# A batch norm's statistics taken out of the opening stage and placed among the steps of the first super tile

## The chip, the cores and the metric

One Trainium2 chip; the program runs on one of its cores. The metric is the device time of an execution in microseconds (us), smaller being better. The engines are TensorE (PE; PEld is its weight load), VectorE (DVE), ScalarE (ACT), GpSimd (POOL), and SyncE (SP), which issues most DMA transfers. Each engine works through its own instructions in order and waits on semaphores for the others.

## The reference

Two layers over x of shape (2, 2048, 256), in float32. The first adds two branches to x, both fed by a layer norm: a state space block, and a mixture of small experts found by product keys. The part that the change touches is the batch norm in front of the key search:

```python
xn = _layernorm(x, axis=-1)
x = x + _L0_attn_ref(xn, ...) + _L0_ffn_ref(xn, ...)
...
q = (hidden_states @ Wq + bq).reshape(B, S, H, QD)      # in _L0_ffn_ref, hidden_states = xn
mean = q.mean(axis=(0, 1, 2))
var = q.var(axis=(0, 1, 2))
q = (q - mean) / jnp.sqrt(var + EPS_BN) * bn_gamma + bn_beta
q0 = _l2norm(q[..., :HALF])
q1 = _l2norm(q[..., HALF:])
```

The mean and variance run over all 4096 rows and 8 heads, so they must be known before the first query is normalised. The state space block normalises xn a second time. The second layer is causal attention plus a mixture of 8 routed experts.

## The kernel before

The 4096 rows are 32 tiles of 128 rows (`NT`), four tiles to a super tile (`TPS`), eight super tiles (`NST`). All of x stays in on-chip memory (`xr`).

**The opening stage** (lines 235 to 464) holds its scratch tiles in one pool (`s_k`) and its matmul results in two others. Instead of computing all queries twice, it gathers the Gram matrix of the normalised rows, of 256 x 256 with a column of sums, and derives the queries' mean and variance from it:

- `measured(t)` (line 285): VectorE takes mean and variance of the rows of a tile.
- `scaled(st)` (294): GpSimd turns them into scale s1 and bias b1 of the first layer norm, four small instructions for each super tile.
- `products(st)` (301): ScalarE writes the normalised rows of four tiles into one of two buffers xg, and TensorE adds their products to two accumulators, psg (L309) and psh (L310).
- `scaled_twice(st)` (312): GpSimd computes scale s2 and bias b2n for the second normalisation, and s1p, in seven instructions with a scratch tile r2 (L316 to L322).
- `powers()` (335): a generator whose steps, small matmuls with VectorE copies, build the powers of the state matrix; its later steps build lt (L360, L365) and bw (L370, L374). One step is taken after every second tile of `measured`.

The loop over super tiles (387) calls `measured` and a `powers` step for the tiles of super tile st, then `scaled(st)`, then `products(st - 1)`. Within this stage the order on TensorE, VectorE, ScalarE and GpSimd is the order written. Behind the loop come a memset of a 128 x 2064 region of zeros (`zero`, a part of the tile xnT1 that is not used yet; line 403), `scaled_twice` for the first four super tiles, the keys' transpose (408), and then the batch norm's chain (413 to 464):

- gm (414, 415): the accumulators scaled; its missing block by a transpose (417, 418);
- wgw (423, 426): gm times the query weights, times the weights;
- psm (432, 436): 32 one-column matmul pieces, which give mean and second moment by column;
- mq, dev, acc1 (442 to 447), a matmul that averages over the heads (449), the deviations (451 to 455), a second such matmul (457), the root on GpSimd (459), and bn_a, bn_b (462 to 464), which `queries_taken` (729) uses.

The other four `scaled_twice` stand behind the root on GpSimd. Behind the stage SyncE sends `zero` five times to a buffer in device memory (467).

**The super tiles' stage.** Every step of a super tile is a small function with a start time in a table (`PLAN`, and `ENDING` for the last super tile). `at(st, f, ...)` (493) puts it on a list with the time st * 68.0 + start, and the sorted list (1483) is the order of TensorE, VectorE, ScalarE and GpSimd; the times only sort. The opening of super tile 0 reads: `rows_twice` (ScalarE, with s2 and b2n), `rows_twice_turned` (TensorE transposes, L193), `rows_twice_taken` (ScalarE, into xn2T), `x_part` (TensorE, L553, xn2T times the input weights), `inputs` (L541), `ends` (L594), `scan_round` (L606), and further on `queries` (L725). New pools, `l0_k` for scratch among them, are opened for this stage in the memory that the opening stage's pools give back.

Of the kernel before, what the change touches and what calls it, by code (L numbers as in the profile page):

```python
# [9 lines left out]
F32 = mybir.dt.float32  # L10
I32 = mybir.dt.int32
AF = mybir.ActivationFunctionType
ALU = mybir.AluOpType
AX = mybir.AxisListType
# [3 lines left out]
P = 128  # L18
B, L, D = 2, 2048, 256
T = B * L  # L20
NT = T // P
SW = 512
NST = T // SW
TPS = SW // P
SPB = L // SW
EPS = 1e-5

DI, DS, DC = 512, 16, 4
NI = DI // P
# [23 lines left out]
    products=((82.01, 79.31), (94.08, 92.53), (114.32, 113.41), (129.20, 128.99)),  # L53
# [6 lines left out]
ZW = 2064  # L60
RW = D + 2
NOROW = 1.0 * 2 ** 20

ENDING = dict(
    rows_twice=(-41.22, -13.33, -40.66, -17.29), rows_twice_turned=(-6.87, 0.70), rows_twice_taken=(-0.20, 1.41),
# [32 lines left out]
PH, PQ, PK = 8, 64, 32  # L98
# [19 lines left out]
PP_GAMMA, PP_BETA, PP_CW, PP_CB, PP_BQ, PP_BNG, PP_BNB, PP_RB, PP_QROW, PP_B1 = 0, 2, 4, 20, 24, 28, 29, 30, 34, 38  # L118
PP_N = PP_B1 + E * NF

M_ID, M_TRI, M_ONE, M_MASK, M_AVG, M_SEL = range(6)
# [3 lines left out]
def layers_kernel(  # L125
# [32 lines left out]
    V, S, G, PE = nc.vector, nc.scalar, nc.gpsimd, nc.tensor  # L158
# [8 lines left out]
    mats = keep.tile([P, 6, P], F32, name="mats")  # L167
    pp = keep.tile([P, PP_N], F32, name="pp")
    small = keep.tile([P, 20 + NT], F32, name="small")
    nhalf = keep.tile([P, 64], F32, name="nhalf")  # L170
# [9 lines left out]
    ident = mats[:, M_ID, :]  # L180

    def col(c, n=1):
        return pp[:, c:c + n]
# [12 lines left out]
    with tc.tile_pool(name="xt", bufs=1) as xt:  # L196

        xnT1 = xt.tile([P, 2, T], F32, name="xnT1")


        with ExitStack() as c3, ExitStack() as c2, ExitStack() as c1:
# [5 lines left out]
            wq_sb = mp.tile([P, 2, PH * PQ], F32, name="wq_sb")  # L207
# [12 lines left out]
            bn_a = wp.tile([P, 1], F32, name="bn_a")  # L220
            bn_b = wp.tile([P, NI], F32, name="bn_b")
# [13 lines left out]
            with ExitStack() as c0:  # L235
                wk = c0.enter_context(tc.tile_pool(name="s_k", bufs=1))
                ps1 = c0.enter_context(tc.tile_pool(name="s_p1", bufs=1, space=PSUM))
                ps2 = c0.enter_context(tc.tile_pool(name="s_p2", bufs=2, space=PSUM))
# [62 lines left out]
                def products(st):  # L301
                    for t in range(st * TPS, (st + 1) * TPS):
                        a = xg[st % 2][:, t % TPS, :]
                        S.activation(
                            a[:, 0:D], xr[:, t, :], AF.Identity, bias=b1[:, t:t + 1], scale=s1[:, t:t + 1]
                        )
                    for t in range(st * TPS, (st + 1) * TPS):
                        a = xg[st % 2][:, t % TPS, :]
                        PE.matmul(psg, a[:, 0:P], a, start=(t == 0), stop=(t == NT - 1))  # L309
                        PE.matmul(psh, a[:, P:D], a[:, P:], start=(t == 0), stop=(t == NT - 1))  # L310

                def scaled_twice(st):

                    ts, m, v, h = of_tile(st)
                    r2 = wk.tile([P, TPS], F32, name="r2", bufs=2)
                    G.tensor_tensor(r2, v, s1[:, ts], ALU.mult)  # L316
                    G.tensor_tensor(r2, r2, s1[:, ts], ALU.mult)
                    G.tensor_scalar(r2, r2, EPS, None, ALU.add)
                    G.tensor_tensor(r2, r2, h, ALU.pow)
                    G.tensor_tensor(s2[:, ts], s1[:, ts], r2, ALU.mult)  # L320
                    G.tensor_tensor(b2n[:, ts], b1[:, ts], r2, ALU.mult)
                    G.tensor_scalar(s1p[:, ts], s1[:, ts], 1.0, None, ALU.add)  # L322
# [61 lines left out]
                kt = wk.tile([P, P], F32, name="kt")  # L384
                k2 = wk.tile([P, 1], F32, name="k2")
                todo = powers()
                for st in range(NST + 1):
                    for t in range(st * TPS, min(st + 1, NST) * TPS):
                        measured(t)
                        if t % 2:  # L390
                            next(todo, None)
                    if st < NST:
                        scaled(st)
                    if st:
                        products(st - 1)
                    if st == NST - 2:
                        V.tensor_tensor(kt, kn, kn, ALU.mult)
                        V.tensor_reduce(k2, kt, AX.X, ALU.add)
                        V.tensor_scalar(k2, k2, 1e-24, None, ALU.max)
                        G.tensor_tensor(k2, k2, nhalf[:, 0:1], ALU.pow)  # L400
                for _ in todo:
                    pass
                G.memset(zero, 0.0)
                for st in range(NST // 2):
                    scaled_twice(st)
                V.tensor_scalar(kn, kn, k2, None, ALU.mult)
                ps = ps1.tile([P, SW], F32, tag="mm", name="ps_mm")
                PE.transpose(ps[:, :P], kn, ident)
# [1 line left out]

                gm = wk.tile([P, 2, D + 1], F32, name="gm")
                V.tensor_scalar(gm[:, 0, :], psg, 1.0 / T, None, ALU.mult)
                V.tensor_scalar(gm[:, 1, P:], psh, 1.0 / T, None, ALU.mult)
                ps = ps1.tile([P, SW], F32, tag="mm", name="ps_mm")
                PE.transpose(ps[:, :P], gm[:, 0, P:D], ident)
                V.tensor_copy(gm[:, 1, 0:P], ps[:, :P])
                wgw = wk.tile([P, 2, PH * PQ], F32, name="wgw")
                for o in range(2):  # L420
                    ps = ps2.tile([P, SW], F32, tag="h", name="ps_gw")
                    for dc in range(2):
                        PE.matmul(
                            ps, gm[:, dc, o * P:(o + 1) * P], wq_sb[:, dc, :], start=(dc == 0), stop=(dc == 1)
                        )
                    V.tensor_tensor(wgw[:, o, :], ps, wq_sb[:, o, :], ALU.mult)
                psm = ps1.tile([P, 2 * NI], F32, tag="st", name="ps_st")
                one = mats[:, M_ONE, 0:1]
                for m in range(NI):
                    ms = slice(m * P, (m + 1) * P)  # L430
                    for dc in range(2):
                        PE.matmul(
                            psm[:, m:m + 1], wq_sb[:, dc, ms], gm[:, dc, D:], start=(dc == 0), stop=(dc == 1)
                        )
                    for dc in range(2):
                        PE.matmul(
                            psm[:, NI + m:NI + m + 1], wgw[:, dc, ms], one, start=(dc == 0), stop=(dc == 1)
                        )
                mq = wk.tile([P, 2 * NI], F32, name="mq")
                acc1 = wk.tile([P, 4], F32, name="acc1")  # L440
                dev = wk.tile([P, NI], F32, name="dev")
                V.tensor_copy(mq, psm)
                V.tensor_tensor(dev, mq[:, 0:NI], mq[:, 0:NI], ALU.mult)
                V.tensor_tensor(mq[:, NI:], mq[:, NI:], dev, ALU.subtract)
                V.tensor_scalar(mq[:, NI:], mq[:, NI:], 0.0, None, ALU.max)
                V.tensor_tensor(mq[:, 0:NI], mq[:, 0:NI], col(PP_BQ, NI), ALU.add)
                V.tensor_reduce(acc1[:, 0:1], mq[:, 0:NI], AX.X, ALU.add)
                ps = ps1.tile([P, 2 * NI], F32, tag="st", name="ps_st")
                PE.matmul(ps[:, 0:1], mats[:, M_AVG, :], acc1[:, 0:1], start=True, stop=True)
                mean = wk.tile([P, 1], F32, name="mean")  # L450
                V.tensor_copy(mean, ps[:, 0:1])
                V.tensor_scalar(dev, mq[:, 0:NI], mean, None, ALU.subtract)
                V.tensor_tensor(dev, dev, dev, ALU.mult)
                V.tensor_tensor(dev, dev, mq[:, NI:], ALU.add)
                V.tensor_reduce(acc1[:, 1:2], dev, AX.X, ALU.add)
                ps = ps1.tile([P, 2 * NI], F32, tag="st", name="ps_st")
                PE.matmul(ps[:, 0:1], mats[:, M_AVG, :], acc1[:, 1:2], start=True, stop=True)
                V.tensor_scalar(acc1[:, 2:3], ps[:, 0:1], EPS, None, ALU.add)
                G.tensor_tensor(acc1[:, 2:3], acc1[:, 2:3], nhalf[:, 0:1], ALU.pow)
                for st in range(NST // 2, NST):  # L460
                    scaled_twice(st)
                V.tensor_tensor(bn_a, acc1[:, 2:3], col(PP_BNG), ALU.mult)
                V.tensor_scalar(bn_b, col(PP_BQ, NI), mean, bn_a, ALU.subtract, ALU.mult)
                V.tensor_scalar(bn_b, bn_b, col(PP_BNB), None, ALU.add)

            for n in range(E * CAP * RW // (P * ZW)):
                nc.sync.dma_start(buf_z[n], zero)
# [23 lines left out]
            plan = []  # L491

            def at(st, f, *args):
                start = (PLAN if st < NST - 1 else ENDING)[f.__name__]
                for n in args:
                    start = start[n]
                plan.append((st * PERIOD + start, len(plan), f, args))

            def mamba(st):
                b = st // SPB  # L500
# [1185 lines left out]
```

## Time and profile before

| | before |
|---|---|
| median of 4 runs | 2087.78 us |
| lowest to highest | 2084.13 to 2089.53 us |
| profiled execution, its own time | 2087.93 us |
| its span | 2086.2 us |
| instructions | 38155 |
| TensorE busy | 2023.2 us, 97% of the span |
| VectorE, ScalarE, GpSimd busy | 1443.3, 1069.4, 598.2 us |
| keys' transpose on TensorE | 45.90 us |
| first `x_part` of super tile 0 | 61.16 us |

A row of the timeline gives the start in us, the duration, the engine, the line, the operation, the tile written and those read, the shape, how often it was repeated and, in brackets, how long the engine stood idle before it and what released it. Times on TensorE are pipelined: one matmul may start before the listed end of the one ahead, so distances of starts say more than durations. The granted clock is TensorE's, as a share of full speed.

### The profile page before, as it was taken

What the parts mean: (1) busy time and instruction counts of PE and PEld (TensorE: products, weight loads), DVE (VectorE), ACT (ScalarE), POOL (GpSimd) and SP (SyncE); (2) the same over time, 40 slices, a digit from 0 to 9 for tenths busy, and PEclk for the clock granted to TensorE, in tenths of its full rate; (3) what the DMA queues carried; (4) which work ended last, traced back from release to release, by engine and by line L of the source; (5) the groups of instructions that cost most, each with busy time, mean ns of one, the idle gap of its engine ahead of it and who ended that gap; (6) DMA issues with size and microseconds to landing.
All of it is one profiled execution on the core that took longest, in us unless ns stands there. A gap on an engine that the chain in (4) does not pass through costs nothing. (4 is left out here: it accounts for less than half of the span.)

```text
span 2086.2 us, 38155 instructions
## 1 busy us (share of the span) xinstructions
PE 2023.2 (97%) x14094; PEld 1031.5 (49%) x14094; DVE 1443.3 (69%) x4920; ACT 1069.4 (51%) x2028; POOL 598.2 (29%) x971
## 2 busy tenths in 40 slices
PE   7999999999979999999999999999999999999997
PEld 6455666565544343433333333433333333678786
DVE  4288898888996887777877788878878773211110
ACT  4576777676611345545555655565555657221211
POOL 5234555446573301310211102111011010332321
PEclk9999999999976999999999999999999999999999
DMA  6000000000121401210110101101200001433320
GB/s 230 28 1 1 11 6 6 11 11 9 39 89 49 91 7 42 60 25 32 33 30 17 45 27 43 37 17 26 75 10 10 7 10 49 144 116 101 111 72 13
DMA packets 64731, 90.82 MB, mean 44 GB/s; under 512 B 19640, under 2 KB 47606, under 8 KB 62880
## 3 DMA queue, kind: packets, MB, share of 16 engines
q1 hardware_dynamic: 58960, 76.75, 12.7%
q0 software_dynamic: 5376, 10.59, 1.6%
q8 instruction: 110, 1.80, 0.4%
q10 hardware_dynamic: 208, 1.05, 0.2%
q14 instruction: 77, 0.63, 0.1%
HBM read 56.53 MB, written 32.02 MB: 42 GB/s over the span
## 5 line engine op out<-in xcount | busy, mean ns | idle before, releaser
L1280 ACT ACTIVATE pt<-ps_p 128x512 f32<-128x512 f32 (+3 forms) x1280 | 608.1, 532 | 501.9 <-PE ps_p L1232 347.8
L1232 PE MATMUL ps_p<-kT,qT 32*128 32x512 f32 (+3 forms) x2560 | 717.2, 585 | 7.0 <-DVE mx L1243 6.0
L1275 PE MATMUL ps_p<-qT,kT 32*128 32x512 f32 (+3 forms) x2560 | 630.5, 575 | 1.7 <-DVE t L1150 0.8
L1248 DVE TENSOR_REDUCE mx<-ps_p 128x1 f32<-128x512 f32 x768 | 491.7, 685 | 133.6 <-PE ps_p L1232 93.5
L1282 POOL TENSOR_SCALAR_AFFINE_SELECT pt<-pt 128x128 f32<-128x128 f32 x512 | 143.8, 292 | 808.9 <-ACT pt L1280 800.7
L1300 PE MATMUL ps_av<-pt,va 128*32 128x256 f32 (+1 forms) x4608 | 351.8, 379 | 4.0 <-POOL pt L1282 2.8
L1275 PEld LDWEIGHTS ps_p<-qT,kT 32*128 32x128 f32 x2560 | 204.7, 184 | 231.4 <-issue 170.3
L1232 PEld LDWEIGHTS ps_p<-kT,qT 32*128 32x128 f32 x2560 | 257.0, 186 | 46.1 <-ACT pt L1280 22.6
L1300 PEld LDWEIGHTS ps_av<-pt,va 128*32 128x32 f32 x4608 | 92.3, 108 | 375.8 <-issue 210.2
L1243 DVE CUSTOM_DVE_ANT_0 ps_p<-ps_p,mask_w 128x384 f32<-128x384 f32 (+3 forms) x512 | 241.4, 515 | 52.6 <-PE ps_p L1232 37.2
L1564 ACT ACTIVATE hT<-ps_h,pp 128x640 f32<-128x640 f32 x64 | 50.8, 794 | 222.1 <-PE ps_h L1560 222.1
L1578 PE MATMUL ps_eo<-w_sb,hT 128*128 128x256 f32 x640 | 141.8, 379 | 0.0
L1560 PE MATMUL ps_h<-xeT,w_sb 128*128 128x320 f32 x512 | 139.1, 432 | 0.0
L1578 PEld LDWEIGHTS ps_eo<-w_sb,hT 128*128 128x128 f32 x640 | 120.5, 190 | 16.7
L553 PE MATMUL ps_mm<-xn2T,w_in_sb 128*128 128x512 f32 x256 | 124.0, 607 | 0.0
L1560 PEld LDWEIGHTS ps_h<-xeT,w_sb 128*128 128x128 f32 x512 | 97.2, 190 | 39.6
L1582 DVE SCALAR_TENSOR_TENSOR eo<-ps_eo,xe,rs 128x256 f32<-128x256 f32 x40 | 19.4, 484 | 135.2 <-PE ps_eo L1578 135.2
L849 POOL TENSOR_TENSOR prod<-prod 128x1024 f32<-128x1024 f32 x32 | 75.2, 2351 | 82.8 <-DVE prod L839 80.6
L811 DVE MATCH_REPLACE8 mr<-m,sc 128x36 f32<-128x36 f32 x512 | 84.9, 176 | 0.0
L1583 POOL DMA_INDIRECT out_x<-eo,row x40 | 39.4, 985 | 151.5 <-DVE eo L1582 141.6
L839 DVE TENSOR_TENSOR prod<-e,ex 128x1024 f32<-128x1024 f32 x64 | 79.4, 1262 | 0.3
L1243 DVE DVE_READ_ACCUMULATOR2_ANT mx<- 128x1 f32 x512 | 72.6, 142 | 0.1
(270 smaller groups left out, 2528.7 us busy)
## 6 DMA issues: line engine op xcount, KB each, us to landing
w_sb<-in_w SPq DMA_DIRECT2D x16, 1024.0 KB
qk_d<-rot SPq DMA_DIRECT2D x16, 512.0 KB
tab<-in_c_tab SPq DMA_DIRECT2D x8, 768.0 KB
buf<-xnT SPq DMA_DIRECT2D x5, 1032.0 KB
xe<-buf SPq DMA_DIRECT2D x8, 645.0 KB
xr<-in_x SPq DMA_DIRECT2D x8, 512.0 KB
res<-xr SPq DMA_DIRECT2D x8, 512.0 KB
out_x<-xr SPq DMA_DIRECT2D x8, 512.0 KB
```

The source lines that it names most:

```text
L553: PE.matmul(ps, w_in_sb[:, dc, m * P:(m + 1) * P], h["xn2T"][:, dc], start=(dc == 0), stop=(dc == 1))
L811: V.match_replace(out=mr[:, g, :], in_to_replace=h["m8", k][:, g, :], in_values=sc2[k % 2][:, g, :], imm_value=GONE,)
L839: V.tensor_tensor(prod, h["e0", k][:, hs, :].unsqueeze(3).to_broadcast([P, PH // 2, 8, PK]), h["e4", k][:, hs, 1, :].unsqueeze(2).to_broad ...
L1232: PE.matmul(ps[:, :w], qT[u][r, qt * P:(qt + 1) * P], kT[u][r, kc * SW:kc * SW + w], start=True, stop=True)
L1243: V.tensor_tensor_reduce(out=ps[:, :w], in0=ps[:, :w], in1=a["mask"][:, SW - w:], scale=1.0, scalar=2 * MASKED, op0=ALU.add, op1=ALU.max, ...
L1248: V.tensor_reduce(to, ps[:, :w], AX.X, ALU.max)
L1275: PE.matmul(ps[:, c0:], kT[u][r, kt * P:(kt + 1) * P], qT[u][r, qb * SW + c0:(qb + 1) * SW], start=True, stop=True,)
L1280: S.activation(p[:, c0:], ps[:, c0:], AF.Exp, scale=HD ** -0.5)
L1282: G.affine_select(out=p[:, c0:c0 + P], in_=p[:, c0:c0 + P], pattern=[[1, P]], compare_op=ALU.is_ge, fill=0.0, base=0, channel_multiplier=-1,)
L1300: PE.matmul(av[u, qb][32 * j:32 * j + 32, lo:hi], va_of(b, g)[:, kt, v0:v0 + 32], pt[n, j][:, lo:hi], start=(kt == half == 0), stop=(kt == ...
L1560: PE.matmul(ps[:, hf, :HC], w1_sb[:, dc, f * P:(f + 1) * P], xeT[:, dc, hf * HC:(hf + 1) * HC], start=(dc == 0), stop=(dc == 1),)
L1578: PE.matmul(ps, hT[:, f, c * P:(c + 1) * P], w2_sb[:, f, :], start=(f == 0), stop=(f == NF - 1))
```

## The change

Two things. In the loop, `products` is called two super tiles behind `measured`, not one. And the batch norm's chain behind the scaling of the accumulators leaves the opening stage: its steps become fourteen entries of the list of super tile 0, with start times of their own (`NORM`). gm and wgw now lie in regions of xnT1 that are not used yet; mq, dev, acc1 and mean are tiles of the pool `l0_k`, and the matmul results take buffers of the super tiles' stage. All eight `scaled_twice` stand in a row behind the loop, ahead of the memset of `zero`.

```diff
+NORM = (-9.0, -8.9, -8.8, -8.7, -8.6, -8.5, -8.4, -1.0, -0.9, 2.9, 3.0, 11.0, 11.7, 13.0)
 ...
-                for st in range(NST + 1):
-                    for t in range(st * TPS, min(st + 1, NST) * TPS):
+                for st in range(NST + 2):
+                    for t in range(min(st, NST) * TPS, min(st + 1, NST) * TPS):
                         measured(t)
 ...
-                    if st:
-                        products(st - 1)
+                    if st > 1:
+                        products(st - 2)
 ...
+                for st in range(NST):
+                    scaled_twice(st)
                 G.memset(zero, 0.0)
-                for st in range(NST // 2):
-                    scaled_twice(st)
 ...
-                gm = wk.tile([P, 2, D + 1], F32, name="gm")
+                gm = xnT1[:, 0, T - 2 * (D + 1):].rearrange("p (a b) -> p a b", a=2)
                 V.tensor_scalar(gm[:, 0, :], psg, 1.0 / T, None, ALU.mult)
                 V.tensor_scalar(gm[:, 1, P:], psh, 1.0 / T, None, ALU.mult)
-                ps = ps1.tile([P, SW], F32, tag="mm", name="ps_mm")
-                PE.transpose(ps[:, :P], gm[:, 0, P:D], ident)
 ...
-                for st in range(NST // 2, NST):
-                    scaled_twice(st)
 ...
+            wgw = xnT1[:, 0, T - 2 * (D + 1) - 2 * PH * PQ:T - 2 * (D + 1)].rearrange("p (a b) -> p a b", a=2)
+            bn = {}
+            def norm_turned():
+                ps = bn["t"] = ps1.tile([P, TPS, P], F32, tag="ms", name="ps_ms")
+                PE.transpose(ps[:, 0, :], gm[:, 0, P:D], ident)
+            def norm_taken():
+                V.tensor_copy(gm[:, 1, 0:P], bn["t"][:, 0, :])
+            def norm_products(o):
+                ps = bn[o] = ps2.tile([P, SW], F32, tag="q", name="ps_q")
+                for dc in range(2):
+                    PE.matmul(ps, gm[:, dc, o * P:(o + 1) * P], wq_sb[:, dc, :], start=(dc == 0), stop=(dc == 1))
+            def norm_weighted(o):
+                V.tensor_tensor(wgw[:, o, :], bn[o], wq_sb[:, o, :], ALU.mult)
+            def norm_columns(sq):
 ...
+                        w, v = (wgw[:, dc, ms], one) if sq else (wq_sb[:, dc, ms], gm[:, dc, D:])
+                        PE.matmul(bn["s"][:, sq, m:m + 1], w, v, start=(dc == 0), stop=(dc == 1))
+            def norm_mean():
+                mq = bn["mq"] = wk.tile([P, 2, NI], F32, name="mq")
+                dev = bn["dev"] = wk.tile([P, NI], F32, name="dev")
+                acc1 = bn["acc"] = wk.tile([P, 4], F32, name="acc1")
+                V.tensor_copy(mq, bn["s"])
 ...
+            def norm_over(n):
+                ps = bn["a", n] = ps1.tile([P, 2, NI], F32, tag="ms", name="ps_ms")
+                PE.matmul(ps[:, 0, 0:1], mats[:, M_AVG, :], bn["acc"][:, n:n + 1], start=True, stop=True)
+            def norm_deviation():
 ...
+            def norm_root():
+                acc1 = bn["acc"]
+                V.tensor_scalar(acc1[:, 2:3], bn["a", 1][:, 0, 0:1], EPS, None, ALU.add)
+                G.tensor_tensor(acc1[:, 2:3], acc1[:, 2:3], nhalf[:, 0:1], ALU.pow)
+            def norm_end():
 ...
+            for n, (f, *args) in enumerate((
+                (norm_turned,), (norm_taken,), (norm_products, 0), (norm_weighted, 0), (norm_products, 1),
+                (norm_weighted, 1), (norm_columns, 0), (norm_columns, 1), (norm_mean,), (norm_over, 0),
+                (norm_deviation,), (norm_over, 1), (norm_root,), (norm_end,),
+            )):
+                plan.append((NORM[n], len(plan), f, args))
```

Where a part is left out, the instructions are those of the lines removed. For super tile 0 the table has `rows_twice_turned` at -10.60 and 1.40, `rows_twice_taken` at -0.64 and 2.93, `x_part` from 10.92, `inputs` at 11.85 and `ends` at 16.71.

More of the change, by code (lines that the diff above doesn't have):

```diff
@@ L409, in layers_kernel @@
                 V.tensor_copy(kb, ps[:, :P])
-                gm = wk.tile([P, 2, D + 1], F32, name="gm")
+                gm = xnT1[:, 0, T - 2 * (D + 1):].rearrange("p (a b) -> p a b", a=2)
                 V.tensor_scalar(gm[:, 0, :], psg, 1.0 / T, None, ALU.mult)
                 V.tensor_scalar(gm[:, 1, P:], psh, 1.0 / T, None, ALU.mult)
-                ps = ps1.tile([P, SW], F32, tag="mm", name="ps_mm")
-                PE.transpose(ps[:, :P], gm[:, 0, P:D], ident)
-                V.tensor_copy(gm[:, 1, 0:P], ps[:, :P])
@@ L419, in layers_kernel @@
[L419 to L459, printed above, removed]
-                for st in range(NST // 2, NST):
-                    scaled_twice(st)
-                V.tensor_tensor(bn_a, acc1[:, 2:3], col(PP_BNG), ALU.mult)
@@ L463, in layers_kernel @@
-                V.tensor_scalar(bn_b, col(PP_BQ, NI), mean, bn_a, ALU.subtract, ALU.mult)
-                V.tensor_scalar(bn_b, bn_b, col(PP_BNB), None, ALU.add)
             for n in range(E * CAP * RW // (P * ZW)):
@@ new lines, in norm_weighted @@
+            def norm_weighted(o):
+                V.tensor_tensor(wgw[:, o, :], bn[o], wq_sb[:, o, :], ALU.mult)
+            def norm_columns(sq):
+                if not sq:
+                    bn["s"] = ps1.tile([P, 2, NI], F32, tag="ms", name="ps_ms")
+                one = mats[:, M_ONE, 0:1]
+                for m in range(NI):
+                    ms = slice(m * P, (m + 1) * P)
+                    for dc in range(2):
+                        w, v = (wgw[:, dc, ms], one) if sq else (wq_sb[:, dc, ms], gm[:, dc, D:])
+                        PE.matmul(bn["s"][:, sq, m:m + 1], w, v, start=(dc == 0), stop=(dc == 1))
@@ new lines, in norm_mean @@
+            def norm_mean():
[3 more added lines that the diff above has]
+                V.tensor_copy(mq, bn["s"])
+                V.tensor_tensor(dev, mq[:, 0, :], mq[:, 0, :], ALU.mult)
+                V.tensor_tensor(mq[:, 1, :], mq[:, 1, :], dev, ALU.subtract)
+                V.tensor_scalar(mq[:, 1, :], mq[:, 1, :], 0.0, None, ALU.max)
+                V.tensor_tensor(mq[:, 0, :], mq[:, 0, :], col(PP_BQ, NI), ALU.add)
+                V.tensor_reduce(acc1[:, 0:1], mq[:, 0, :], AX.X, ALU.add)
@@ new lines, in norm_over @@
+            def norm_over(n):
+                ps = bn["a", n] = ps1.tile([P, 2, NI], F32, tag="ms", name="ps_ms")
+                PE.matmul(ps[:, 0, 0:1], mats[:, M_AVG, :], bn["acc"][:, n:n + 1], start=True, stop=True)
+            def norm_deviation():
+                mq, dev = bn["mq"], bn["dev"]
+                mean = bn["mean"] = wk.tile([P, 1], F32, name="mean")
+                V.tensor_copy(mean, bn["a", 0][:, 0, 0:1])
+                V.tensor_scalar(dev, mq[:, 0, :], mean, None, ALU.subtract)
+                V.tensor_tensor(dev, dev, dev, ALU.mult)
+                V.tensor_tensor(dev, dev, mq[:, 1, :], ALU.add)
+                V.tensor_reduce(bn["acc"][:, 1:2], dev, AX.X, ALU.add)
@@ new lines, in norm_root @@
+            def norm_root():
[3 more added lines that the diff above has]
+            def norm_end():
+                V.tensor_tensor(bn_a, bn["acc"][:, 2:3], col(PP_BNG), ALU.mult)
+                V.tensor_scalar(bn_b, col(PP_BQ, NI), bn["mean"], bn_a, ALU.subtract, ALU.mult)
+                V.tensor_scalar(bn_b, bn_b, col(PP_BNB), None, ALU.add)
```

## The prediction

> **What bounds the kernel now.** I read the page first: its engine times and its 40 slices.
>
> ```profile
> PE 2023.2 (97%) x14094; PEld 1031.5 (49%) x14094; DVE 1443.3 (69%) x4920; ACT 1069.4 (51%) x2028; POOL 598.2 (29%) x971
> ...
> PE   7999999999979999999999999999999999999997
> ...
> PEclk9999999999976999999999999999999999999999
> ```
>
> TensorE is busy in every slice except the first and last, so time is lost where TensorE stands still or runs at a low clock. The table by stage (busy time of PE, PEld, DVE, ACT, POOL, then granted clock) finds the stage that the change touches:
>
> ```profile
> 0.00:46.00 46.00, 33.02 (x197) 28.36 (x197) 21.05 (x105) 21.69 (x44) 21.80 (x66) 0.93 0.64 204
> 46.00:58.26 12.26, 8.70 (x47) 6.31 (x46) 4.41 (x18) 0.71 (x2) 5.78 (x19) 0.86 0.80 334
> 58.26:68.00 9.74, 8.84 (x35) 3.88 (x35) 1.02 (x5) 5.30 (x12) 8.30 (x26) 0.65 0.01 2
> 68.00:120.00 52.00, 52.00 (x206) 28.41 (x206) 24.25 (x99) 35.28 (x58) 8.95 (x12) 1.00 0.00 1
> ```
>
> The batch norm's chain is the second row, super tile 0's opening the third. From 68 us TensorE is busy 52.00 of 52.00 us at clock 1.00, and in the changed program every instruction and wait behind super tile 0's first steps is the old one. So what the opening gains or loses up to 68 us goes to the end one for one. TensorE's own order there (timeline):
>
> ```profile
> 45.90 0.27 PE L408 MATMUL ps_mm<-mats,kn 128*128 128x128 f32 x1
> ...
> 53.91 0.58 PE L436 MATMUL ps_st<-mats,wgw 128*128 128x1 f32 x4
> 55.70 0.56 PE L449 MATMUL ps_st<-acc,mats 128*128 128x1 f32 x2 [1.20 <-DVE acc L447]
> 57.36 0.59 PE L457 MATMUL ps_st<-acc,mats 128*128 128x1 f32 x2 [1.10 <-DVE acc L455]
> 58.29 1.09 PE L193 MATMUL ps_tp<-mats,xn 128*128 128x128 f32 x4 [0.34 <-DVE acc L458]
> 60.25 1.12 PE L193 MATMUL ps_tp<-mats,xn 128*128 128x128 f32 x4 [0.87 <-ACT xn2T L521]
> 61.16 3.62 PE L553 MATMUL ps_mm<-xn2T,w_in_sb 128*128 128x512 f32 x4
> 64.71 1.12 PE L541 MATMUL ps_v<-xn2T,bw 128*32 128x128 f32 x16
> ```
>
> Brackets are waits for VectorE's four-column steps and, at L193, for ScalarE's copy. Last, VectorE and GpSimd:
>
> ```profile
> 33.23 0.19 DVE L374 COPY bw<-ps_mm 128x32 f32<-128x32 f32 x1 [2.03 <-PE ps_mm L370]
> ...
> 40.29 0.24 POOL L299 TENSOR_SCALAR b<-b 128x4 f32<-128x4 f32 x1
> 40.47 1.82 POOL L403 MEMSET xnT<- 128x2064 f32 x1
> 42.26 0.20 POOL L316 TENSOR_TENSOR r<-mv,s 128x4 f32<-128x4 f32 x1
> ...
> 44.40 0.20 POOL L321 TENSOR_TENSOR b2n<-b,r 128x4 f32<-128x4 f32 x1
> ...
> 44.88 0.20 POOL L316 TENSOR_TENSOR r<-mv,s 128x4 f32<-128x4 f32 x1
> ```
>
> One `scaled_twice` starts 2.62 us after another (42.26, 44.88; 47.48 and 50.07 follow), and its b2n ends 2.34 us in.
>
> **Part 1: the chain inside the plan, without waits.** The changed order on TensorE is: keys' transpose, transposes of super tile 0 (dc 0), `norm_turned`, `norm_products`, `norm_columns`, transposes (dc 1), `norm_over(0)`, `x_part(0)`, `norm_over(1)`, `inputs`. No instruction is saved; what can go are the stalls. Counting from the keys' transpose at 45.90: it lasts 0.11 us on its engine and VectorE's kb and two gm steps end at 47.03, so the transposes start at 47.2; 0.55 us at full clock (half of 1.09) and 0.13 for `norm_turned`: 47.9. Eight 512-column pieces at 0.43 (47.05 to 50.49): 51.35. Thirty-two one-column pieces at 0.111 (four in 0.45 us): 54.9. Transposes dc 1: 55.5. `norm_mean` takes 1.17 us from mq's copy (54.53) to L449's start (55.70), plus 0.1: `norm_over(0)` at 56.2, `x_part(0)` at 56.5. That is 4.65 us ahead of 61.16.
>
> **Part 2: the wait that is added.** mq, dev and acc1 are now allocated in the pool that opens after the first stage, over the first stage's scratch memory, where GpSimd keeps r2. In the changed program as built, VectorE's copy into mq waits on GpSimd's counter at the value set by b2n of the eighth `scaled_twice`. All eight now stand in one row behind the last `scaled`, where before only four stood ahead of the chain and the copy (54.53) waited for TensorE alone. Queued behind the copy on VectorE is the rest of the chain; TensorE stands in `norm_over(0)`, with `x_part(0)` and all of super tile 0 behind it.
>
> GpSimd's end, P: the last `scaled` ends at 40.53; the zero memset (1.82 us) no longer follows at once. Seven sets at 2.60 plus 2.34 make 20.54 us. With the old start P would be 61.07. The start moves, because lt and bw stand behind products of three super tiles on TensorE instead of four, and VectorE measures the last eight tiles behind bw's copy. One super tile's products took 2.82 us (25.83 to 28.65). Against this, products of super tile 0 start about 1.2 us later (behind two more `powers` steps that follow VectorE's pace), while the gap of 0.76 us (16.63 to 17.39) behind them goes: 2.4 us earlier. Bounds: 3.6, if bw's 16 pieces run at full clock (1.8 by the column price, not 3.0), and 1.1, if a super tile's products fall to half clock (+1.3, half of 2.6). I take 2.4, the rows as they are: the start at 38.1, P = 58.65 (57.45 to 59.95).
>
> Products end about where they did: bw's pieces end at 30.6 instead of 33.04, and five super tiles at 2.62 plus the 2.3 us that half clock cost from 33.04 to 37.68 make 46.0 (43.7 at full clock, 47.5 with more half clock). The column work ends at 55 (52.7 to 56.5), ahead of P in all cases, so a later end of products is covered by this same wait; without it each microsecond there would count in full.
>
> From P: 0.1 + 1.17 gives `norm_over(0)` at 59.9, a wait of 3.7 us against 56.2. Its pair takes 0.3 at half clock: `x_part(0)` at 60.2, four pieces at 0.86 until 63.6, `norm_over(1)` until 63.9. Then the clock decides.
>
> ```profile
> 54.00:55.00 1.00, 0.50 (x5) 0.41 (x4) 0.40 (x3) 0.00 (x0) 0.00 (x0) 0.87 0.95 396
> ...
> 64.00:65.00 1.00, 1.00 (x9) 0.26 (x12) 0.00 (x0) 0.19 (x1) 0.75 (x4) 0.51 0.00 0
> ```
>
> It fell at 54.74 (from the row's mean of 0.87), after one-column matmuls that had kept TensorE 1.00 busy, and came back at 64.98, 3.8 us after `x_part(0)` began; before, it fell at 30.86 (row 30 to 31: 0.93) and came back at 37.68 (0.66), 4.6 us after products resumed. These changes lie 6.82, 17.06 and 10.24 us apart, near 2, 5 and 3 times 3.41: I read steps of 3.4 us. With its return at 64.98 as before, `inputs` runs 1.1 us at half clock and 0.45 at full: `x_part(1)` at 65.4 instead of 65.76. The gain is 0.3 to 0.7; I take 0.5. If the clock stays up, 1.9 us more are gained (half of x_part's 3.4 and the pairs); one step later costs half of it, 1.7.
>
> [...]
>
> **What is moved at no cost.** The zero memset and its five transfers start near 58.9 instead of 40.47 and 42.32; no transfers ran from 60 to 90, and their reader, `sent` of super tile 0, is planned 216 us in. GpSimd then has 1.82 and 1.09 (L481) until 61.8; `norm_root`'s power is asked of it only after `norm_over(1)`, at 64.2. bn_a waits for that power (0.6), and behind it on VectorE stand the hx copies, due at the scan's first round (72.07 before): seven us of cover; uncovered it would cost its 0.6. SP's queue holds nothing else until the attention's loads. ScalarE's first `rows_twice` now lies among its last xg writes (0.5 us each), ready for TensorE by 43 to 46; uncovered, 1.5 us.
>
> **The sum.** The profiled execution took 2087.93 us (span 2086.2 and 1.73 around it), against a median of 2087.78. 2087.93 - 0.5 = 2087.4. From both bounds, P (-1.2, +1.3) and clock (-1.9, +1.7): 2084.3 to 2090.4. Four runs of before differ by 5.4 us, so about 0.2% (4.2 us) is the least that a measurement can tell from no change.
>
> **Rivals.** *The overlap works* (0.20): GpSimd is done before the columns are, P below 54.9. Then part 1 holds: 2087.93 - 4.65 = 2083.3, with the clock 2081.4 to 2085.0. For it: VectorE alone could finish measuring by some 28 us. Against it: bw's copy cannot pass three super tiles of products, and 20.54 us of GpSimd follow.
>
> *GpSimd starts no earlier* (0.18, the slower side): half clock in the products ahead of bw eats the 2.4 us, P = 61.07, `x_part(0)` at 62.6, 1.4 late, and the clock's return a step later, 1.7: 2089.4 to 2091.1. It decides once the first `scaled_twice` starts after 39.5. [...]
>
> *The chain isn't in the plan at all in effect*: that is the forecast (0.62), since its VectorE half waits as if outside.
>
> **Chances.** The bound for slower, 2092.1, lies above all three cases, and the one for faster, 2083.7, within the first rival; the rest is the spread of the runs. The forecast gives 0.03 faster, 0.56 same, 0.03 slower; the first rival 0.14 faster, 0.06 same; the second 0.11 same, 0.07 slower: 0.17, 0.73, 0.10. Leaving out a tenth on each side, the range is 2083.0 to 2090.8.
>
> **What would show it.** Right: mq's copy is released by GpSimd's b2n near 58.7, TensorE stands some 3 to 4 us in `norm_over(0)`, clock 0.50 follows, `x_part(0)` starts near 60.2, the zero transfers near 59. Wrong: the copy released by TensorE near 55, or bw's copy no earlier than 33.2.

## The result, and the profile after

The changed kernel takes 2091.94 us (median of 43 runs, 2086.24 to 2095.84), the kernel before, on the same chips, 2086.96 us (66 runs, 2083.34 to 2091.93). The ratio is 1.0018, with an interval of 1.0013 to 1.0023: about 3.8 us slower (the ratio weighs all runs; the medians lie 4.98 us apart). The forecast of 2087.4 and its range, which ended at 2090.8, both lie below the median. The profiled execution took 2093.02 us, with a span of 2091.2 us and a clock of 0.974 (before: 2087.93, 2086.2, 0.977).

The stage table of the kernel after, in the columns of the one before (stretch and its length, busy time of PE, PEld, DVE, ACT, POOL, then granted clock, DMA share, GB/s):

```profile
0.00:46.00 46.00, 32.16 (x187) 27.61 (x187) 21.02 (x105) 23.57 (x45) 22.84 (x72) 0.89 0.57 178
46.00:58.26 12.26, 9.94 (x61) 7.46 (x59) 2.50 (x6) 2.06 (x4) 10.28 (x36) 0.98 0.01 1
58.26:68.00 9.74, 4.97 (x20) 2.80 (x24) 4.18 (x12) 1.79 (x6) 4.53 (x8) 0.51 0.59 243
68.00:120.00 52.00, 52.00 (x206) 27.63 (x200) 23.11 (x94) 34.15 (x57) 6.59 (x6) 1.00 0.14 57
```

In the second row TensorE does more than before (9.94 us for 8.70): the chain without stalls. In the third it does less (4.97 for 8.84), and half of the stretch is a standstill. TensorE's timeline says where (in brackets the idle time ahead of a group, and what ended it):

```profile
47.53 0.27 PE L410 MATMUL ps_mm<-mats,kn 128*128 128x128 f32 x1
...
56.31 0.64 PE L195 MATMUL ps_tp<-mats,xn 128*128 128x128 f32 x4
63.02 0.56 PE L495 MATMUL ps_ms<-acc,mats 128*128 128x1 f32 x2 [6.08 <-DVE acc L491]
63.44 3.76 PE L577 MATMUL ps_mm<-xn2T,w_in_sb 128*128 128x512 f32 x4
...
68.40 1.98 PE L577 MATMUL ps_mm<-xn2T,w_in_sb 128*128 128x512 f32 x4
```

L195 is the second set of transposes, L495 `norm_over`, L577 `x_part`. All independent work is done at 56.9; then TensorE stands for 6.08 us in `norm_over(0)`, which waits for VectorE's L491. `x_part(1)` starts at 68.40 instead of 65.76, 2.64 us late. VectorE's timeline follows that wait back:

```profile
31.77 0.19 DVE L376 COPY bw<-ps_mm 128x32 f32<-128x32 f32 x1 [1.57 <-PE ps_mm L372]
...
59.59 0.17 DVE L486 COPY mq<-ps_ms 128x8 f32<-128x8 f32 x1 [5.88 <-POOL b2n L323]
60.18 2.50 DVE L489 TENSOR_SCALAR mq<-mq 128x4 f32<-128x4 f32 x1
60.26 2.42 DVE L490 TENSOR_TENSOR mq<-mq,pp 128x4 f32<-128x4 f32 x1
62.72 0.16 DVE L491 TENSOR_REDUCE acc<-mq 128x1 f32<-128x4 f32 x1
```

Two things stand there. The copy into mq was released by GpSimd's b2n: the wait that the prediction named. And L489, a maximum with zero over four columns, took 2.50 us. In the kernel before, the same step is this line:

```profile
55.13 0.17 DVE L445 TENSOR_SCALAR mq<-mq 128x4 f32<-128x4 f32 x1
```

L490 is queued behind it: both end at 62.68. The reader of such a row must not take 2.50 us for work; a step of 0.17 us shown 15 times as long was held up while it was running. What ran beside it is in GpSimd's timeline:

```profile
39.04 0.20 POOL L318 TENSOR_TENSOR r<-mv,s 128x4 f32<-128x4 f32 x1
...
59.36 0.20 POOL L323 TENSOR_TENSOR b2n<-b,r 128x4 f32<-128x4 f32 x1
59.64 0.23 POOL L324 TENSOR_SCALAR s1p<-s 128x4 f32<-128x4 f32 x1
59.81 1.82 POOL L407 MEMSET xnT<- 128x2064 f32 x1
61.57 1.09 POOL L434 MEMSET sc<- 128x576 f32 x2
```

The first `scaled_twice` starts at 39.04, b2n of the eighth ends at 59.56, and the memset of `zero` and those of sc run from 59.81 to 62.66. L489 ends with the last of them.

### The profile page after: what moved, and what is told of

Its sections match the earlier page's. It is cut to its first block, busy times and chain, and to the rows that moved or that the text cites. A ratio compares the mean times of both kernels' runs of the same rounds, so it can differ in the third digit from the quotient of the medians.

```text
span 2091.2 us, 38151 instructions
## 1 busy us (share of the span) xinstructions
PE 2024.9 (97%) x14094; PEld 1032.2 (49%) x14094; DVE 1445.2 (69%) x4920; ACT 1070.7 (51%) x2028; POOL 597.6 (29%) x971
## 5 line engine op out<-in xcount | busy, mean ns | idle before, releaser
L577 PE MATMUL ps_mm<-xn2T,w_in_sb 128*128 128x512 f32 x256 | 124.2, 608 | 0.0
```

The source lines that it names most:

```text
L577: PE.matmul(ps, w_in_sb[:, dc, m * P:(m + 1) * P], h["xn2T"][:, dc], start=(dc == 0), stop=(dc == 1))
```

## The experiments

The theory: GpSimd's wait is what was forecast, and the missing microseconds are L489, held up by the memsets. The rivals: the lag of two super tiles costs by itself; the lateness is that of GpSimd's start; the difference arises later, from the clock. One mark serves for all of them: the first matmul of `norms`, the next stage of super tile 0, at 99.61 us before and at 102.24 after (+2.63, the whole delay of `x_part(1)`).

**The lag alone.** The kernel before with

```diff
-for st in range(NST + 1):
-    for t in range(st * TPS, min(st + 1, NST) * TPS):
+for st in range(NST + 2):
+    for t in range(min(st, NST) * TPS, min(st + 1, NST) * TPS):
-    if st:
-        products(st - 1)
+    if st > 1:
+        products(st - 2)
```

> The kernel before with products two super tiles behind their measures, and nothing else of the change. Marker: the first matmul of `norms` (99.61 us before, 102.24 after the change), which no later change of the clock can move. Theory A (the whole loss is GpSimd's part in the batch norm's chain, but the lag has a cost of its own, 1.63 us at the keys' transpose, 45.90 to 47.53): keys' transpose near 47.5, marker near 101.2, time about 1.5 us over before. Theory B (the lag is neutral, the later products hide behind something): marker within 0.5 of 99.6, time within 0.5 us of before.

2089.1 us against 2087.36, ratio 1.0012 [1.0004, 1.0021]. The lag costs by itself. The keys' transpose, the first matmul behind all products, stands at 48.25 (45.90 before), and the mark at 101.9:

```profile
48.25 0.27 PE L408 MATMUL ps_mm<-mats,kn 128*128 128x128 f32 x1
```

That transpose varies between profiles: 46.22 to 48.25 in the seven with a lag of two, 45.90, 46.39 and 46.91 in the three with a lag of one. The 2.35 us of this pair are the far end of the spread; the ratio is the better measure. Besides, a load of x landed late in this profile:

```profile
10.53 0.43 DVE L287 BATCH_NORM_STATS2 ln_stats<-xr 128x6 f32<-128x256 f32 x1 [2.02 <-DMA xr<-in_x]
```

VectorE waits 2.02 us for it there (not at all in the kernel before, 0.54 us in the changed one), and what follows in the stage is late by it, GpSimd too: the memset of `zero` starts at 40.78, not ahead of the 40.47 of before. So the profile doesn't tell how much of its 2.35 us, or of its mark, is the lag's.

**The chain alone.** The changed kernel with the old loop (a lag of one).

> The changed kernel with products one super tile behind, as before: the chain's move alone. Theory A (VectorE's copy into mq waits for the eighth `scaled_twice`, then a 128x4 step of VectorE stands still until GpSimd's two memsets are over): the last b2n ends near 61.1, as GpSimd starts at 40.5; the memsets end near 64.2 and the 128x4 maximum with them; `x_part(0)` starts near 64.9, marker near 103.7, time 4 us or more over before. Theory B (the products' lag is the loss): marker near 99.6 or below.

2092.01 us, ratio 1.0022 [1.0011, 1.0033]; the mark at 103.9 (+4.3).

```profile
64.73 0.56 PE L495 MATMUL ps_ms<-acc,mats 128*128 128x1 f32 x2 [8.76 <-DVE acc L491]
```

The eighth b2n now ends at 61.26, 1.70 us later than with the lag of two, and L489 again takes 2.50 us (61.88 to 64.38), to the end of the memsets. So inside this change the lag does bring GpSimd forward, as the prediction had it: the first `scaled_twice` starts at 38.27 to 39.30 in the six profiles of the changed program with a lag of two, at 40.74 and 41.20 in the two with a lag of one. That is worth 1.7 us at the mark (103.9 to 102.2), while by itself the lag costs. The two ratios, 1.0022 and 1.0018, don't tell the versions apart.

**The wait taken away.** mq, dev, acc1 and mean as tiles of another pool, `wp`, which leaves the copy into mq no wait on GpSimd:

```diff
-mq = bn["mq"] = wk.tile([P, 2, NI], F32, name="mq")
+mq = bn["mq"] = wp.tile([P, 2, NI], F32, name="mq")
```

> The changed kernel with mq, dev, acc1 and mean in the long-lived pool that holds bn_a and bn_b, so that the copy into mq no longer waits for the end of the first stage's scratch memory. Theory A (that wait and what follows from its lateness are the whole stall in `norm_over(0)`): the copy starts within 0.3 us of the last one-column matmul (near 56.5), `x_part(0)` near 58, marker near 96.8 (1.7 either way by the clock), time about 5 us under the changed kernel and 1 to 4 us under before. Theory B (TensorE would wait there for something else, or VectorE's small steps are slow beside GpSimd): `x_part(0)` later than 61, marker above 100.

2084.34 us, ratio 0.9988 [0.9976, 0.9999]; the mark at 96.5, 3.1 us ahead of the kernel before.

```profile
55.49 0.17 DVE L486 COPY mq<-ps_ms 128x8 f32<-128x8 f32 x1 [2.77 <-PE ps_ms L480]
56.09 0.17 DVE L489 TENSOR_SCALAR mq<-mq 128x4 f32<-128x4 f32 x1
```

TensorE releases the copy now, L489 runs 3 us ahead of the memsets and takes its 0.17 us, and TensorE waits 0.72 us in `norm_over(0)`. This is the prediction's first rival (the overlap works), brought about by where four small tiles lie.

**The blocked step behind other work.** In the changed kernel, the last five times of `NORM`, so that `norm_over(0)` stands behind both `x_part` and `inputs`:

```diff
-..., -1.0, -0.9, 2.9, 3.0, 11.0, 11.7, 13.0)
+..., -1.0, -0.9, 16.8, 16.9, 18.7, 18.8, 19.0)
```

> The changed kernel with other start times for the chain's last six steps: `norm_over(0)` 16.8, `norm_deviation` 16.9, `norm_over(1)` 18.7, `norm_root` 18.8, `norm_end` 19.0, so that `x_part(0)`, `inputs`, `x_part(1)` and `ends` stand ahead of `norm_over(0)` on TensorE. The wait of VectorE for GpSimd stays. Theory A (the wait costs only because `norm_over(0)` stands ahead of `x_part(0)` on TensorE): `x_part(0)` starts near 57.5, the copy into mq still near 59.6 and the maximum still ends near 62.7; marker near 97.5, time 3 to 5 us under the changed kernel. Theory B (VectorE's lateness reaches TensorE all the same, by v_sb or hx behind the chain): marker above 100.

2083.97 us, ratio 0.9985 [0.9973, 0.9996]; the mark at 95.6 (-4.0). The copy still waits for b2n (59.71) and L489 still takes 2.50 us, but `x_part(0)` starts at 55.96 and all that reaches TensorE is this, in `ends`:

```profile
63.25 0.39 PE L618 MATMUL ps_e<-v_sb,lt 128*16 128x128 f32 x2 [1.07 <-DVE v_sb L572]
```

Beyond this 1.07 us, the wait costs time only because `norm_over(0)` stands ahead of `x_part(0)`.

**The same value by another form of instruction.** L489 as a maximum of two tensors, the second a tile of zeros:

```diff
-V.tensor_scalar(mq[:, 1, :], mq[:, 1, :], 0.0, None, ALU.max)
+V.tensor_tensor(mq[:, 1, :], mq[:, 1, :], cnt[1][:, 0, 0:NI], ALU.max)
```

> The changed kernel with one instruction in another form: the maximum with zero over 128x4 is a tensor-tensor maximum against a tile of zeros instead of a tensor-scalar one. It took 2.50 us in the changed kernel and ended with GpSimd's memsets (62.66). Theory A (a tensor-scalar step of VectorE from and to on-chip memory can't run beside a GpSimd memset, while a step with two such inputs can): it takes 0.16 us, `norm_over(0)` starts near 60.8 instead of 63.0, the marker (first matmul of `norms`, 102.24) falls to about 99.9, and the time by some 2 us. Theory B (any step of VectorE would have stood still there): it takes 2.4 us again and the marker stays at 102.2.

2087.54 us against 2088.26, ratio 0.9995 [0.9981, 1.0009]: no difference from before, and an interval wholly below that of the changed kernel (1.0013 to 1.0023). One instruction in another form takes the loss back. The mark is at 99.5.

```profile
59.85 0.16 DVE L489 TENSOR_TENSOR mq<-mq,cnt 128x4 f32<-128x4 f32 x1
61.22 1.14 DVE L501 TENSOR_SCALAR dev<-mq,mean 128x4 f32<-128x4 f32 x1
...
59.48 1.82 POOL L407 MEMSET xnT<- 128x2064 f32 x1
61.24 1.09 POOL L434 MEMSET sc<- 128x576 f32 x2
```

At the same place, on the same tile, 0.37 us into the memset of `zero` (59.48 to 61.30), the step takes 0.16 us. The next tensor-scalar step, L501, is the one that is held, from 61.22 to 62.36, where the memsets of sc end at 62.33. It was 0.23 us where no memset ran beside it (63.81 in the changed kernel). TensorE waits 3.67 us in `norm_over(0)` and `x_part(0)` starts at 60.84.

**One memset less.** `G.memset(zero, 0.0)` ahead of the loop and so of the scaling, in a single run.

> The changed kernel with the memset of `zero` moved to the start of the loop, where GpSimd has nothing to do; GpSimd then has only the memsets of sc (1.09 us) behind the eighth `scaled_twice`. Theory A (the maximum waits for whichever memset runs): it ends with the memsets of sc, near 61.0, after 0.7 us instead of 2.50; marker near 100.5. Theory B (its 2.50 us have another cause): 2.5 us again, marker 102.2.

2090.58 us for the one run (span 2088.7), which is inside the spread of the kernel before and says little; the mark is at 100.3.

```profile
60.05 0.75 DVE L489 TENSOR_SCALAR mq<-mq 128x4 f32<-128x4 f32 x1
```

L489 again ends with the memsets (60.80; those of sc run from 59.68 to 60.78), and is 1.75 us shorter because the memset of 1.82 us is gone from there. Both kinds of memset count: the step pays what is left of them when it starts (0.75 us here, 2.50 with both).

**All of it together.** Own pool, the memset of `zero` first, the later times, and a lag of one:

> The changed kernel with four edits: mq, dev, acc1 and mean in the long-lived pool, `zero` set first, the last six steps of the chain later (16.8 to 19.0), products one super tile behind as before. Theory A (all that was lost lay in these waits, and the lag is worth nothing or less once GpSimd's end no longer counts): `x_part(0)` near 55.5, marker near 94.8, time 4 to 6 us under before. Theory B (the lag of two is worth its place): the next kernel is faster by 1 us or more.

2078.82 us, ratio 0.9953 [0.9938, 0.9968]: the fastest version, ahead of both kernels, and its slowest run (2082.96) is ahead of the fastest of before in that comparison (2083.19). The mark is at 94.9, and from 58.26 to 68 us TensorE is busy 9.74 of 9.74 us, at a clock of 0.94 (before 8.84 and 0.65, changed 4.97 and 0.51).

**The same with a lag of two.**

> As the kernel before in this list, with products two super tiles behind. Theory A: keys' transpose 0.6 to 1.6 us later than with one, and the marker later by as much, near 95.5 to 96.4. Theory B: marker and time at or below the kernel with one.

2081.73 us, ratio 0.9969 [0.9957, 0.9981]. The mark is at 94.6, which is no later than with a lag of one, though a later mark was expected. The keys' transpose is 1.12 us later, as expected (48.03 for 46.91); the clock, at 1.00 from 46 to 68 us against 0.91 and 0.94 in the two stretches, makes up for it. Yet the median is 2.9 us higher. The intervals overlap, so a cost of the lag is likely here, not shown.

What the mark says and what the medians say, as differences from the kernel before in us:

| version | mark | ratio x 2087, with its interval |
|---|---|---|
| chain alone | +4.3 | +4.6 (2.3 to 6.9) |
| changed kernel | +2.6 | +3.8 (2.7 to 4.8) |
| lag alone | +2.3 | +2.5 (0.8 to 4.4) |
| maximum of two tensors | -0.1 | -1.0 (-4.0 to 1.9) |
| own pool | -3.1 | -2.5 (-5.0 to -0.2) |
| later times | -4.0 | -3.1 (-5.6 to -0.8) |
| all together, lag of two | -5.0 | -6.5 (-9.0 to -4.0) |
| all together, lag of one | -4.7 | -9.8 (-12.9 to -6.7) |

The mark comes from one profile and lies inside the interval in six of the eight (that of the lag alone has the late load in it). The changed kernel's lies just outside, and the last row has 5 us that the mark doesn't show.

## Why the prediction was wrong

**Right: what bounds, and where.** From 68 us TensorE is busy 52.00 of 52.00 us again, and the 2.64 us that the opening lost stand unchanged at the first `norms` (2.63). The cause of the wait was right, too: GpSimd's eighth b2n released the copy. Taking that wait away gave the first rival's case, 2084.34 us against 2083.3.

**Nearly right: P.** It was 59.56 instead of 58.65, inside the bounds of 57.45 to 59.95. Seven sets and a b2n took 20.52 us (39.04 to 59.56) where 20.54 were reckoned; the whole error is the start, 39.04 instead of 38.1. bw's copy came 1.46 us earlier (31.77 for 33.23), not 2.4, because the clock was down in the products ahead of it: the rows from 23 to 27 us have 0.76, 0.50, 0.50 and 0.53, where those of before have 1.00. The second rival named this half clock; it came, in part. A second cause is smaller: VectorE waited 0.54 us for a load of x (until 8.87), which it didn't before.

**Wrong: "What is moved at no cost".** The prediction asked who reads `zero`, when its transfers run and whose turn on GpSimd it takes, and then listed 2.91 us of memsets as free. It didn't ask what runs on VectorE during them. The forecast itself put the memsets (58.9 to 61.8) over the steps from P to `norm_over(0)`, and sized those steps by `norm_mean`'s 1.17 us from a place where GpSimd was still. The term was 0.1 + 1.17 us and measured 3.46 (from P, 59.56, to 63.02). The sum by steps: `x_part(0)` was to start at 60.2; 0.94 from GpSimd's start and 2.33 from L489 (2.50 - 0.17) make 63.47, and it started at 63.44. With the missed term taken out (the maximum of two tensors) `norm_over(0)` starts 1.20 us behind P (59.23 to 60.43) where 1.27 were reckoned, and the time is that of before: the rest of the sum held. That its bracket says 3.67 us and the forecast 3.7 is chance: the forecast counted from 56.2, the bracket from the end of the transposes.

**The clock.** It fell at 57.66 (the row 57 to 58 has 0.83), 0.7 us after the last transposes, and came back at 67.9, 4.5 us after `x_part(0)` had begun (row 67 to 68: 0.55); 10.24 us lie between, three times the 3.41 us that the prediction read from distances of 6.82, 17.06 and 10.24. The prediction's rows had 3.8 and 4.6. `x_part(1)` followed `x_part(0)` by 4.96 us, where 5.2 were reckoned.

**Open: the rest.** The two profiled executions differ by 5.09 us, of which the opening has 2.64. Adding up, in rows of 10 us from 120 to 2070 us, the clock that was not granted (1 less the clock, by 10) gives 35.9 us before, 39.3 after and 29.0 in the fastest version. The rows that make the difference are the same few places, such as 730 to 740 us, where the clock is 0.97 before (first row) and 0.50 after (second row):

```profile
730.00:740.00 10.00, 10.00 (x92) 3.65 (x85) 7.93 (x20) 6.34 (x12) 0.00 (x0) 0.97 0.08 16
730.00:740.00 10.00, 10.00 (x52) 3.20 (x45) 5.33 (x15) 3.84 (x7) 0.00 (x0) 0.50 0.07 15
```

None of these stages is touched by the change. Runs of one and the same kernel lie 7 to 11 us apart, so it is likely that falls of this kind come and go. Whether an earlier opening makes them rarer, as the fastest version's median suggests, stays open: three other versions with an early opening have 35.8 (own pool), 39.3 (later times) and 35.9 (all together, lag of two), no less than the 35.9 of before.

## What to carry to other kernels

When a step moves to another engine's busy time, look at both engines' rows over the place where it lands: the moved memsets were free for GpSimd and for their readers, and cost 2.33 us on VectorE, in a step of four columns. A tile that is taken from a pool laid over freed scratch memory inherits the last user of that memory, and four tiles of a few columns elsewhere were worth the difference between +3.8 and -2.5 us. A small matmul that waits for another engine belongs behind the independent large ones: that alone turned the same waits into a gain.

## What the runs showed of the hardware

A tensor-scalar step of VectorE with source and result in SBUF that ran beside a memset of GpSimd lasted to the memset's end in the five cases that the profiles hold from 25 to 75 us: L489 2.50 us in the changed kernel, with the chain alone and with the later times, 0.75 with the memset of `zero` first, for a step of 0.17; L501 1.14 with the maximum of two tensors, for one of 0.23. When the next memset followed at once, the waiting step didn't get in between (2.50 us, across 1.82 and 1.09). A tensor-tensor step on the same tile wasn't held (0.16 us, 59.85 to 60.01 within the memset of 59.48 to 61.30, with the maximum of two tensors), nor was a tensor-scalar step of 0.16 us that reads PSUM: this one, in the run with the own pool, lies within the memsets of sc (60.80 to 61.89):

```profile
61.10 0.16 DVE L508 TENSOR_SCALAR acc<-ps_ms 128x1 f32<-128x1 f32 x1 [2.83 <-PE ps_ms L495]
```

It has one column only, so that row doesn't tell whether PSUM or the size spared it. A copy from PSUM of 128 columns was spared, too, in the fastest version with a lag of two, within the memsets of sc (60.08 to 61.18):

```profile
60.53 0.29 DVE L572 COPY v_sb<-ps_v 128x128 f32<-128x128 f32 x1 [2.53 <-PE ps_v L565]
```

The profile shows the held step as busy (2.50 us, without a bracket), not as waiting, and puts TensorE's 6.08 us down to VectorE's L491, not to GpSimd. These rows show which forms were held, and until when; what holds them, no run here shows.
